# Depthwise inputs stored once per shift, loaded by one transfer for four groups, in a four-layer network on one core

## The chip, the cores and the metric

The kernel runs on one core of one Trainium2 chip. The metric is the device time of one execution in microseconds (us). TensorE (PE) multiplies, VectorE (DVE) does elementwise work and scans, ScalarE (ACT) activations, GpSimd (POOL) issues most DMAs here, and SyncE (SP) issues the rest. Everything is float32.

## The reference

Four layers are applied in a row to x of shape (8, 384, 32, 32).

Layer 0 normalises over channels (RMS norm) and runs a selective state-space block forwards and backwards over the 1024 pixels: an input projection to u and z, a causal depthwise 1-d convolution of u with four taps, then a recurrence with 16 states per channel. Beside it stands a 3x3 depthwise convolution of the normalised image.

```
h = dA * h + dBu;  y = sum over states of h * C        # recurrence, per pixel
local = sigmoid(dwconv3x3(x_norm) + b) * x_norm
x1 = x + res_scale * ((fwd + bwd) * scale_mod + local)
```

Layer 1 is a 1x1 convolution, a 3x3 depthwise convolution, another 1x1 convolution with a residual, linear attention with 8 heads, and an MLP of width 1536. Layers 2 and 3 are sums of depthwise convolutions with up to 13x13 taps, a 1x1 convolution between them, and a GELU at the end.

## The kernel before, in words

**The whole.** A head prepares constants. Then `_layers01` treats layers 0 and 1 image by image (8 images, each in two halves of 512 pixels, 384 channels as three blocks of 128). At the end, layers 2 and 3 run over all images with Toeplitz matrices on PE (L249). The change touches only `_layers01`.

**Depthwise convolutions of layers 0 and 1.** They run on PE. A group is 32 channels; a block of 128 channels has four groups. For a group, an input tile holds the same rows several times, each copy shifted by one element: 32 channels x 3 shifts = 96 partitions for the 3x3 kernel, 32 x 4 = 128 for the 1-d one. A matmul with 32 columns sums the shifted copies with their taps; four groups fill the 128 partitions of one PSUM tile (`col32`, L430). The image goes to a DRAM scratch with a zero border first (`put_image`, L449, into `xn_d` and `h_d`; u into `u_d`, L511). The shifts are made by the load: the source pattern `[1, 3]` reads the same scratch row from three neighbouring starts (`conv3`, L460; for u the pattern `[1, 4]`, L548). So a product of 128 channels needs four loads. Their tiles have the tag `im`, with N_IM = 6 buffers. The scratches have two slots, for even and odd images, and are set to zero once in the head (L372).

**The scan.** `scan(b)` has 48 units per image (2 directions x 2 halves x 3 blocks x 4 groups of states). A unit takes four exponentials on ACT (L682), a product (L695), a scan instruction (L702 or L705) and a second product (L617) on DVE, and four matmuls that sum over the states into `acc` (L619). Its work tiles `du` have four buffers.

**Background work.** `front(b+1)` (norm, projections, depthwise convolutions, step sizes) and `layer1(b-1)` are generators. They are advanced between the units of `scan(b)`, so that PE has work beside DVE. Each `yield n` tells the cost of a step; after unit i the loop has brought the background to `need * (i + 1) / 48`, where `need` is the sum of the numbers given beside each generator: 94 for the front, 290 for layer 1, 30 for folding weights. What is left over when the scan ends is run before the next scan. The yields in the code add up, for the front, to 6 + 36 + 18 + 48 = 108, and for layer 1 to 18 + 18 + 18 + 48 + 4 + 18 + 6 + 6 + 18 + 6 + 6 + 144 = 310.

**Deferred DVE work.** `defer(n, fn)` keeps a piece of DVE work back for n ticks, so that DVE does not wait at once for PE and ACT. `residual` (L790) adds the second 1x1 convolution to the image; `last` (L932) adds the MLP.

**Order and queues.** The program is written with a tile framework. A scheduler in it sets the final order of the instructions on each engine from the order of the code and its own estimates; within an engine that order is kept. All loads and stores of the background go through POOL, in order; each takes one of eight semaphores in turn and waits for the transfer that had it before. The scan's loads go through SP. Weight tiles (`wtile`, L399, tag `w`) have five buffers; activations of half an image (tag `a6`) have seven.

Of the kernel before, what the change touches and what calls it, by code (L numbers as in the profile page):

```python
# [8 lines left out]
FP = mybir.dt.float32  # L9
# [5 lines left out]
P = 128  # L15
C = 384
NC = C // P
H = 32
W = 32
L = H * W  # L20
HALF = 512
# [12 lines left out]
SEG = HALF + 1  # L34
IMG = (H + 2) * (W + 2)

N_A6, N_T2, N_W, N_IM = 7, 10, 5, 6
HIMG = H // 2 * (W + 2)
UL = L + 6


_BN = ["bn1", "bn2", "pw", "dwk", "dw1"] + [f"l2_{j}" for j in range(7)]
# [259 lines left out]
def _layers01(tc, nc, B, xv, x2_d, dram, ident, mean_w, eps5, eps6, one, half, minus1, vec, bns, bnt,  # L302
# [12 lines left out]
    with ExitStack() as ctx:  # L315
# [5 lines left out]
        def scratch(shape, name):  # L321
            return dram.tile(shape, FP, tag=name, name=name)

        x1_d = scratch([B, C, L], "x1_d")
        bc_d = scratch([B, 2, 2 * NST, L], "bc_d")
        xn_d = scratch([2, C, IMG], "xn_d")
        h_d = scratch([2, C, IMG], "h_d")
        u_d = scratch([2, C, UL], "u_d")
        z_d = scratch([B, C, L], "z_d")
        ud_d = scratch([B, C, L], "ud_d")  # L330
        yf_d = scratch([B, C, L], "yf_d")
# [29 lines left out]
            nc.gpsimd.tensor_scalar_mul(dgd[:, c, :], ident, vec("D", c))  # L361


        zero = wp.tile([P, HALF], FP, tag="zero", name="zero")
        nc.gpsimd.memset(zero, 0.0)
        for i in range(2):
            for t, n in ((xn_d, IMG), (u_d, UL), (h_d, IMG)):
                pads = t[i].rearrange("(c p) i -> p c i", p=P)
                for c in range(NC):
                    for a in range(0, n, HALF):  # L370
                        e = min(n, a + HALF)
                        nc.gpsimd.dma_start(pads[:, c, a:e], zero[:, 0 : e - a])  # L372


        das = []
# [31 lines left out]
        late = []  # L407

        def defer(n, fn):
            late.append([n, fn])  # L410

        def tick(everything=False):
            for e in list(late):
# [31 lines left out]

        def put_image(t_d, slot, h, t):

            v = t_d[slot].rearrange("(c p) i -> p c i", p=P)
            nc.gpsimd.dma_start(v[:, :, (W + 2) + HIMG * h : (W + 2) + HIMG * (h + 1)], t)  # L449

        def conv3(t_d, slot, h, c, taps, name):

            ims = []
            for j in range(4):
                im = sp.tile([P, 18 * (W + 2)], FP, tag="im", name=f"{name}_i{j}", bufs=N_IM)
                src = bass.AP(
                    t_d.tensor, t_d[slot, 32 * (4 * c + j), 16 * h * (W + 2)].offset,
                    [[IMG, 32], [1, 3], [1, 18 * (W + 2) - 2]],
                )
                nc.gpsimd.dma_start(im[:96, 0 : 18 * (W + 2) - 2], src)  # L460
                ims.append(im.rearrange("p (h w) -> p h w", w=W + 2))
            ps = psum(name)
            col32(
                ps, lambda j, i: taps[:96, (4 * c + j) * 3 + i, :],
                lambda j, i: ims[j][:96, i : i + 16, 0:W], 3,
            )
            return ps

# [6 lines left out]
        def front(b):  # L475

            xn = []
            for h in range(2):
# [15 lines left out]
                put_image(xn_d, b % 2, h, t)  # L494
                xn.append(mid)
                yield 3
            uo = u_d[b % 2].rearrange("(c p) i -> p c i", p=P)
            for e in range(2):
                w = wtile(inproj_t[:, e * C : (e + 1) * C], f"win_{b}_{e}")
                for h in range(2):  # L500
                    t = a6(f"uz_{b}_{e}_{h}")
                    for m in range(NC):
                        ps = psum(f"in_{b}_{e}_{m}_{h}")
                        dense(ps, w, m, xn[h])
                        if e == 0:
                            nc.scalar.copy(t[:, m, :], ps)  # L506
                        else:
                            nc.scalar.activation(t[:, m, :], ps, AF.Silu)
                        yield 3
                    if e == 0:  # L510
                        nc.gpsimd.dma_start(uo[:, :, 3 + h * HALF : 3 + (h + 1) * HALF], t)  # L511
                    else:
                        nc.gpsimd.dma_start(zv[b][:, :, bass.ts(h, HALF)], t)

# [22 lines left out]
            for h in range(2):  # L537
                cols = bass.ts(h, HALF)
                ucs = [a6(f"uc_{b}_{h}_{d}") for d in range(2)]
                for c in range(NC):  # L540
                    uts = []
                    for j in range(4):
                        ut = sp.tile([P, 18 * (W + 2)], FP, tag="im", name=f"ut_{b}_{h}_{c}_{j}", bufs=N_IM)
                        src = bass.AP(
                            u_d.tensor, u_d[b % 2, 32 * (4 * c + j), h * HALF].offset,
                            [[UL, 32], [1, 4], [1, HALF + 3]],
                        )
                        nc.gpsimd.dma_start(ut[:, 0 : HALF + 3], src)  # L548
                        uts.append(ut)
                    for d in range(2):  # L550
                        ps = psum(f"c1_{b}_{h}_{c}_{d}")
                        col32(
                            ps, lambda j, i: t1[:, d * NG + 4 * c + j, :],
                            lambda j, i: uts[j][:, 3 * d : 3 * d + HALF], 1,
                        )
                        nc.scalar.activation(ucs[d][:, c, :], ps, AF.Silu, bias=vec("conv1d_b", c))
                    yield 2
# [200 lines left out]
        def layer1(b):  # L758
# [22 lines left out]
            w = wtile(c2_d, f"c2_{b}")  # L781
            for h in range(2):
                for m in range(NC):
                    ps = psum(f"c2_{b}_{m}_{h}")
                    dense(ps, w, m, dws[h])
                    t = t2(f"c2_{b}_{m}_{h}")
                    nc.scalar.activation(t, ps, AF.Identity, bias=biasc[:, m, :])

                    def residual(o=xx[h][:, m, :], t=t):
                        nc.vector.tensor_add(o, o, t)  # L790

                    defer(0, residual)
                    yield 3


# [263 lines left out]
```

## Time and profile before

| | |
|---|---|
| median of 3 runs | 6316.81 us (6316.02 to 6326.15) |
| the profiled execution | 6308.41 us, span 6306.2 us |
| mean granted PE clock | 0.888 |
| PE / DVE / ACT / POOL busy | 5329.2 / 3995.1 / 2810.4 / 1001.8 us |
| DMA | 945.57 MB, 150 GB/s over the span |
| head, to the first scan instruction | about 216 us |
| scans of images 0 to 7 | about 216 to 4810 us |
| layer 1 of the last image, alone | about 4810 to 5160 us |
| layers 2 and 3 | about 5160 to 6306 us |

In the profile, a group of instructions is named by its line, engine, and "output<-input" tiles: `dw<-dw_i,t3b` is the depthwise product of layer 1, `lc<-lc_i,t` that of layer 0, `c<-ut,t` the 1-d convolution, `c<-dw,c` the second 1x1 convolution of layer 1, `mf` and `mo` the two matmuls of the MLP, `acc<-du` the scan's sum over states. "PE dw <- DMA dw_i: 17.3, 5, 5.4" reads: PE sat idle before `dw` for 17.3 us in total, 5 times, at most 5.4 us, until that DMA had landed.

### The profile page before, as it was taken

The numbers are of one execution on the slowest core, as the hardware profiler recorded it, in microseconds if no ns is written. First come the engines' busy times: TensorE is split into PE (matmuls) and PEld (weight loads), VectorE is DVE, ScalarE is ACT, GpSimd is POOL, SyncE is SP. The second block draws the span as 40 slices with busy tenths as digits, with TensorE's granted clock in tenths as the row PEclk, the third lists the DMA queues.
The fourth block names the chain that finished last, engine by engine and source line by source line (L and its number), as shares of the span: only waits on it lengthen the run. The fifth ranks groups of instructions, "written<-read, shape, count | busy, mean of one in ns | idle before, by whom it ended". The sixth has DMA issues, their size and how long they took to land. (4 is left out here: it accounts for less than half of the span.)

```text
span 6306.2 us, 52769 instructions
## 1 busy us (share of the span) xinstructions
PE 5329.2 (85%) x18670; PEld 2530.5 (40%) x18670; DVE 3995.1 (63%) x2702; ACT 2810.4 (45%) x3908; POOL 1001.8 (16%) x1608
## 2 busy tenths in 40 slices
PE   4755678987988799879978997898978999999999
PEld 1211213332432243223323332333323449994999
DVE  1699987977796789769877987897895100002000
ACT  1656574556465646655564557454443300002000
POOL 4211130023002201220131012101001010000111
PEclk7776778997998799879988998899888999999999
DMA  7654663456346634653464356445434124445444
GB/s 210 221 184 158 207 222 117 152 191 208 102 154 203 203 100 160 199 182 106 159 228 152 123 165 227 136 145 167 130 109 134 45 72 96 97 92 167 97 95 83
DMA packets 690666, 945.57 MB, mean 150 GB/s; under 512 B 378476, under 2 KB 404260, under 8 KB 690404
## 3 DMA queue, kind: packets, MB, share of 16 engines
q0 software_dynamic: 148784, 542.48, 26.5%
q1 hardware_dynamic: 372912, 377.17, 19.9%
q10 hardware_dynamic: 168708, 22.55, 2.3%
q8 instruction: 149, 2.44, 0.2%
q14 instruction: 113, 0.93, 0.0%
HBM read 715.94 MB, written 226.04 MB: 149 GB/s over the span
## 5 line engine op out<-in xcount | busy, mean ns | idle before, releaser
L682 ACT ACTIVATE da<-dlt,neg_a 128x512 f32<-128x512 f32 x1536 | 1001.9, 713 | 967.3 <-DVE du L705 529.0
L695 DVE TENSOR_TENSOR du<-vr,bct 128x2048 f32<-128x2048 f32 x384 | 874.6, 2284 | 16.3 <-DMA vr<-v_d 10.7
L617 DVE TENSOR_TENSOR du<-du,bct 128x2048 f32<-128x2048 f32 x384 | 877.8, 2287 | 3.8
L702 DVE TENSOR_TENSOR_SCAN du<-da,du 128x2052 f32<-128x2052 f32 x192 | 849.3, 4428 | 37.2 <-ACT da L682 34.3
L705 DVE TENSOR_TENSOR_SCAN du<-da,du 128x2052 f32<-128x2052 f32 x192 | 848.3, 4427 | 6.1
L619 PE MATMUL acc<-du,selt 128*32 128x512 f32 x3072 | 613.4, 696 | 224.0 <-DVE du L617 223.4
L923 PE MATMUL mo<-hm,w 128*128 128x512 f32 x1152 | 547.1, 616 | 53.9 <-ACT hm L921 51.2
L421 PE MATMUL mf<-ln,w 128*128 128x512 f32 x1152 | 547.7, 610 | 0.6 <-DVE ln L909 0.6
L249 PE MATMUL cv_b<-xt_b,toep 128*128 128x240 f32 (+6 forms) x2496 | 488.0, 358 | 10.0 <-DMA xt_b<-xp_d 10.0
L249 PE MATMUL cv_a<-xt_a,toep 128*128 128x240 f32 (+6 forms) x2496 | 487.1, 358 | 0.0
L249 PEld LDWEIGHTS cv_b<-xt_b,toep 128*128 128x128 f32 x2496 | 466.5, 190 | 32.0 <-issue 10.8
L249 PEld LDWEIGHTS cv_a<-xt_a,toep 128*128 128x128 f32 x2496 | 465.8, 190 | 21.1
L430 PE MATMUL c<-ut,t 128*32 128x512 f32 x768 | 245.4, 802 | 146.6 <-ACT dl L581 55.6
L430 PE MATMUL dw<-dw_i,t3b 96*32 96x512 f32 x1152 | 274.9, 852 | 111.7 <-DMA dw_i<-h_d 101.9
L923 PEld LDWEIGHTS mo<-hm,w 128*128 128x128 f32 x1152 | 216.2, 194 | 368.5 <-issue 242.1
L430 PE MATMUL lc<-lc_i,t 96*32 96x512 f32 x1152 | 256.1, 836 | 119.6 <-DMA lc_i<-xn_d 116.3
L421 PEld LDWEIGHTS mf<-ln,w 128*128 128x128 f32 x1152 | 217.7, 194 | 316.5 <-issue 313.1
L619 PEld LDWEIGHTS acc<-du,selt 128*32 128x32 f32 x3072 | 100.4, 116 | 573.7 <-DVE du L617 294.6
L264 DVE COPY yt<-cv_a 128x256 f32<-128x256 f32 x48 | 20.4, 425 | 461.6 <-PE cv_a L249 461.6
L682 ACT ACT_TABLE_LOAD x231 | 296.4, 1283 | 9.2 <-DVE du L702 5.3
L921 ACT ACTIVATE hm<-mf,biasf 128x512 f32<-128x512 f32 x192 | 130.4, 687 | 370.9 <-PE mf L421 370.0
L421 PE MATMUL in<-xn,win 128*128 128x512 f32 x576 | 258.9, 604 | 11.2 <-ACT uz L506 10.0
(207 smaller groups left out, 6044.0 us busy)
## 6 DMA issues: line engine op xcount, KB each, us to landing
dlt<-dl_d SPq DMA_DIRECT2D x384, 256.0 KB, 5.7
vr<-v_d SPq DMA_DIRECT2D x384, 256.0 KB, 4.4
bct<-bc_d SPq DMA_DIRECT2D x256, 256.0 KB, 4.1
ut<-u_d POOLq DMA_DIRECT2D x192, 257.5 KB, 4.8
lc_i<-xn_d POOLq DMA_DIRECT2D x192, 228.8 KB, 5.3
dw_i<-h_d POOLq DMA_DIRECT2D x192, 228.8 KB, 4.5
w<-w_d POOLq DMA_DIRECT2D x64, 576.0 KB, 4.7
w<-in_w POOLq DMA_DIRECT2D x64, 576.0 KB, 4.3
```

Source lines behind the costliest of these rows:

```text
L249: nc.tensor.matmul(pv[:, :, lo:hi], tp[:, kx, :], xg[:, :, lo + s : hi + s], start=(i == 0), stop=(i == KS - 1),)
L264: nc.vector.tensor_copy(hold["t"][:, g % GB, :], ps)
L421: nc.tensor.matmul(ps, w[:, k, m * P : (m + 1) * P], rhs[k] if isinstance(rhs, list) else rhs[:, k, :], start=(k == 0), stop=(k == NC - 1),)
L430: nc.tensor.matmul(ps[32 * j : 32 * j + 32, :], lhs(j, i), rhs(j, i), start=(i == 0), stop=(i == taps - 1), skip_group_check=True,)
L617: nc.vector.tensor_mul(dv, dv, cct[:, 1:2, :].to_broadcast([P, 4, HALF]))
L619: nc.tensor.matmul(acc[32 * j : 32 * j + 32, :], selt, dv[:, j, :], start=False, stop=(r == NR - 1), skip_group_check=True,)
L682: nc.scalar.activation(da[:, SEG * j + 1 : SEG * (j + 1)], dlt[:, j, :], AF.Exp, scale=neg_a[:, 4 * c + j, r : r + 1],)
L695: nc.vector.tensor_mul(flat(1)[:, :, 0:HALF], vt, bct[r][:, 0:1, :].to_broadcast([P, 4, HALF]))
L702: nc.vector.tensor_tensor_scan(du[:, s], da[:, s], du[:, s], 0.0, ALU.mult, ALU.add)
L705: nc.vector.tensor_tensor_scan(du[:, s][:, ::-1], da[:, s][:, ::-1], du[:, s][:, ::-1], 0.0, ALU.mult, ALU.add)
L921: nc.scalar.activation(hm, ps, AF.Gelu, bias=biasf[:, NC * i + f, :])
L923: nc.tensor.matmul(acc[m], wb[:, f, m * P : (m + 1) * P], hm, start=(i == 0 and f == 0), stop=(i == FF // C - 1 and f == NC - 1),)
```

## The change

The scratches get one more dimension, the shift. `put_image` stores an image half three times, each time one element earlier; u is stored four times. A load for 128 channels is then one transfer with four groups in the free dimension, and the tag `im` holds tiles four times as large with two buffers. The zero fill covers the larger scratches with 18 transfers of 12 pieces per partition instead of 54. To make room, weights have four buffers instead of five. The numbers given for the background become 108 and 310. The residual add is deferred by one tick more, and forced before the step that reads it.

```diff
-N_A6, N_T2, N_W, N_IM = 7, 10, 5, 6
+N_A6, N_T2, N_W, N_IM = 7, 10, 4, 2
-UL = L + 6
+UL = L + 8
...
-        xn_d = scratch([2, C, IMG], "xn_d")
-        h_d = scratch([2, C, IMG], "h_d")
-        u_d = scratch([2, C, UL], "u_d")
+        xn_d = scratch([2, C, 3, IMG], "xn_d")
+        h_d = scratch([2, C, 3, IMG], "h_d")
+        u_d = scratch([2, C, 4, UL], "u_d")
...
-        zero = wp.tile([P, HALF], FP, tag="zero", name="zero")
+        zero = wp.tile([P, C + NC + 1], FP, tag="zero", name="zero")
...
-            for t, n in ((xn_d, IMG), (u_d, UL), (h_d, IMG)):
-                pads = t[i].rearrange("(c p) i -> p c i", p=P)
+            for t, n in ((xn_d, 3 * IMG), (u_d, 4 * UL), (h_d, 3 * IMG)):
+                pads = t[i].rearrange("(c p) s i -> p c (s i)", p=P)
                 for c in range(NC):
-                    for a in range(0, n, HALF):
-                        e = min(n, a + HALF)
-                        nc.gpsimd.dma_start(pads[:, c, a:e], zero[:, 0 : e - a])
+                    z = n // 12
+                    nc.gpsimd.dma_start(
+                        pads[:, c, :].rearrange("p (a z) -> p a z", z=z),
+                        zero[:, 0:z].rearrange("p (o z) -> p o z", o=1).to_broadcast([P, 12, z]),
+                    )
...
         def defer(n, fn):
-            late.append([n, fn])
+            e = [n, fn]
+            late.append(e)
+            return e
+
+        def force(e):
+            if e in late:
+                late.remove(e)
+                e[1]()
...
         def put_image(t_d, slot, h, t):
 
-            v = t_d[slot].rearrange("(c p) i -> p c i", p=P)
-            nc.gpsimd.dma_start(v[:, :, (W + 2) + HIMG * h : (W + 2) + HIMG * (h + 1)], t)
+            for e in range(3):
+                v = t_d[slot][:, e].rearrange("(c p) i -> p c i", p=P)
+                at = (W + 2) + HIMG * h - e
+                nc.gpsimd.dma_start(v[:, :, at : at + HIMG], t)
...
-            ims = []
-            for j in range(4):
-                im = sp.tile([P, 18 * (W + 2)], FP, tag="im", name=f"{name}_i{j}", bufs=N_IM)
-                src = bass.AP(
-                    t_d.tensor, t_d[slot, 32 * (4 * c + j), 16 * h * (W + 2)].offset,
-                    [[IMG, 32], [1, 3], [1, 18 * (W + 2) - 2]],
-                )
-                nc.gpsimd.dma_start(im[:96, 0 : 18 * (W + 2) - 2], src)
+            n = 18 * (W + 2)
+            im = sp.tile([P, 4, n], FP, tag="im", name=f"{name}_i", bufs=N_IM)
+            src = bass.AP(
+                t_d.tensor, t_d[slot, P * c, 0, 16 * h * (W + 2)].offset,
+                [[IMG, 96], [96 * IMG, 4], [1, n - 2]],
+            )
+            nc.gpsimd.dma_start(im[:96, :, 0 : n - 2], src)
...
-                        nc.gpsimd.dma_start(uo[:, :, 3 + h * HALF : 3 + (h + 1) * HALF], t)
+                        for q in range(4):
+                            at = 3 + h * HALF - q
+                            uo = u_d[b % 2][:, q].rearrange("(c p) i -> p c i", p=P)
+                            nc.gpsimd.dma_start(uo[:, :, at : at + HALF], t)
...
+                    ut = sp.tile([P, 4, 18 * (W + 2)], FP, tag="im", name=f"ut_{b}_{h}_{c}", bufs=N_IM)
+                    src = bass.AP(
+                        u_d.tensor, u_d[b % 2, P * c, 0, h * HALF].offset,
+                        [[UL, P], [P * UL, 4], [1, HALF + 3]],
+                    )
+                    nc.gpsimd.dma_start(ut[:, :, 0 : HALF + 3], src)
...
-                    defer(0, residual)
+                    res[h].append(defer(1, residual))
...
             for t in range(L // P):
                 h, q = divmod(t, HALF // P)
+                for e in res[h]:
+                    force(e)
...
-                work.append((front(b + 1), 94))
+                work.append((front(b + 1), 108))
...
-                work.append((layer1(b - 1), 290))
+                work.append((layer1(b - 1), 310))
```

More of the change, by code (lines that the diff above doesn't have):

```diff
@@ L446, in put_image @@
         def put_image(t_d, slot, h, t):
-            v = t_d[slot].rearrange("(c p) i -> p c i", p=P)
-            nc.gpsimd.dma_start(v[:, :, (W + 2) + HIMG * h : (W + 2) + HIMG * (h + 1)], t)
+            for e in range(3):
+                v = t_d[slot][:, e].rearrange("(c p) i -> p c i", p=P)
+                at = (W + 2) + HIMG * h - e
+                nc.gpsimd.dma_start(v[:, :, at : at + HIMG], t)
         def conv3(t_d, slot, h, c, taps, name):
-            ims = []
-            for j in range(4):
-                im = sp.tile([P, 18 * (W + 2)], FP, tag="im", name=f"{name}_i{j}", bufs=N_IM)
-                src = bass.AP(
-                    t_d.tensor, t_d[slot, 32 * (4 * c + j), 16 * h * (W + 2)].offset,
-                    [[IMG, 32], [1, 3], [1, 18 * (W + 2) - 2]],
-                )
-                nc.gpsimd.dma_start(im[:96, 0 : 18 * (W + 2) - 2], src)
-                ims.append(im.rearrange("p (h w) -> p h w", w=W + 2))
+            n = 18 * (W + 2)
[5 more added lines that the diff above has]
+            nc.gpsimd.dma_start(im[:96, :, 0 : n - 2], src)
+            iv = im.rearrange("p j (h w) -> p j h w", w=W + 2)
             ps = psum(name)
@@ L464, in conv3 @@
                 ps, lambda j, i: taps[:96, (4 * c + j) * 3 + i, :],
-                lambda j, i: ims[j][:96, i : i + 16, 0:W], 3,
+                lambda j, i: iv[:96, j, i : i + 16, 0:W], 3,
             )
@@ L496, in front @@
                 yield 3
-            uo = u_d[b % 2].rearrange("(c p) i -> p c i", p=P)
             for e in range(2):
@@ L540, in front @@
                 for c in range(NC):
[L541 to L549, printed above, removed]
+                    ut = sp.tile([P, 4, 18 * (W + 2)], FP, tag="im", name=f"ut_{b}_{h}_{c}", bufs=N_IM)
[4 more added lines that the diff above has]
+                    nc.gpsimd.dma_start(ut[:, :, 0 : HALF + 3], src)
                     for d in range(2):
@@ L553, in front @@
                             ps, lambda j, i: t1[:, d * NG + 4 * c + j, :],
-                            lambda j, i: uts[j][:, 3 * d : 3 * d + HALF], 1,
+                            lambda j, i: ut[:, j, 3 * d : 3 * d + HALF], 1,
                         )
@@ L781, in layer1 @@
             w = wtile(c2_d, f"c2_{b}")
+            res = [[], []]
             for h in range(2):
```

## The prediction

> **What bounds the kernel now.** First the page's busy times, then the windows image by image, then one image cut finer, then its waits, and last the head.
>
> ```profile
> PE 5329.2 (85%) x18670; PEld 2530.5 (40%) x18670; DVE 3995.1 (63%) x2702; ACT 2810.4 (45%) x3908; POOL 1001.8 (16%) x1608
> ```
> ```profile
> 0.00:216.00 216.00, 108.62 (x329) 33.77 (x331) 35.25 (x109) 63.96 (x88) 94.31 (x165) 0.78 0.73 227
> 216.00:696.00 480.00, 275.21 (x921) 81.29 (x918) 468.47 (x299) 274.78 (x388) 73.70 (x128) 0.68 0.54 179
> ...
> 2479.00:3092.00 613.00, 522.57 (x1654) 190.55 (x1656) 492.24 (x315) 343.36 (x468) 103.63 (x173) 0.88 0.51 164
> ...
> 4298.00:4810.00 512.00, 435.51 (x1362) 165.71 (x1354) 451.41 (x262) 244.83 (x340) 52.21 (x80) 0.90 0.41 130
> 4810.00:5160.00 350.00, 324.01 (x904) 136.55 (x904) 33.40 (x45) 75.39 (x109) 42.43 (x65) 0.93 0.24 72
> ```
> Columns: window, length, busy PE, PEld, DVE, ACT, POOL, then PE clock, DMA share, GB/s. Scan 0 is DVE alone (468 of 480). Scans 1 to 6 take about 605 each (2479 to 3092 is the fifth, image 4) with PE 522 and DVE 492: neither is full; each waits for the other in turn. (Scan b runs beside the front of image b+1 and layer 1 of image b-1.) A scan unit needs 2.284 + 2.287 + 4.428 = 9.0 us of DVE, 48 units 432; the other 60 are background work, and some 115 to 120 us an image are DVE stalls. Where?
>
> ```profile
> 2508.00:2552.00 44.00, 43.22 (x117) 17.43 (x116) 16.08 (x15) 15.76 (x23) 8.62 (x12) 1.00 0.44 132
> ...
> 2600.00:2640.00 40.00, 26.36 (x115) 6.78 (x117) 31.23 (x23) 19.58 (x22) 9.26 (x17) 0.67 0.77 227
> ...
> 2680.00:2730.00 50.00, 38.64 (x98) 10.70 (x99) 23.08 (x27) 44.30 (x62) 17.70 (x35) 0.73 0.65 229
> ...
> 2780.00:2830.00 50.00, 39.51 (x124) 13.43 (x120) 26.83 (x14) 15.72 (x25) 6.26 (x12) 0.83 0.51 143
> ...
> 2980.00:3030.00 50.00, 44.35 (x112) 17.48 (x110) 48.17 (x26) 27.16 (x35) 5.26 (x7) 0.93 0.35 106
> ```
> ```profile
> PE dw L430 <- DMA dw_i<-h_d: 17.3, 5, 5.4
> PE lc L430 <- DMA lc_i<-xn_d: 16.2, 5, 5.5
> ...
> DVE xx L932 <- PE mo L923: 23.8, 1, 23.8
> ...
> DVE xx L790 <- ACT c L787: 19.9, 6, 10.4
> ```
> Three places. (1) The image's start: PE is full (43.2 of 44) with MLP steps left over from the previous image, and DVE waits 23.8 us in one piece for `mo`. (2) The depthwise stretches, 2600 to 2830: PE has holes of 33 us, waiting for `lc_i` and `dw_i`, at a clock of 0.67 to 0.83. (3) The residual adds. From 2830 on both engines are nearly full. The bare cost of a depthwise product is seen in the last image, where no scan runs:
>
> ```profile
> 4876.66 6.10 PE L430 MATMUL dw<-dw_i,t3b 96*32 96x512 f32 x24 [2.20 <-DMA dw_i<-h_d]
> 4884.15 6.39 PE L430 MATMUL dw<-dw_i,t3b 96*32 96x512 f32 x24 [1.39 <-DMA dw_i<-h_d]
> 4892.32 5.49 PE L430 MATMUL dw<-dw_i,t3b 96*32 96x512 f32 x24 [1.77 <-DMA dw_i<-h_d]
> ```
> A period of 7.7 us: 6.0 of matmul and 1.8 of waiting. The head:
>
> ```profile
> 36.00:78.00 42.00, 4.37 (x6) 1.17 (x4) 2.27 (x4) 5.25 (x8) 34.72 (x65) 0.59 0.88 270
> ```
> ```profile
> 78.56 1.67 ACT L485 ACTIVATE sq<-xi 128x512 f32<-128x512 f32 x3 [28.86 <-DMA xi<-in_x]
> ```
> ```profile
> lc_i<-xn_d POOLq DMA_DIRECT2D x192, 228.8 KB, 5.3
> xn_d<-xn POOLq DMA_DIRECT2D x16, 816.0 KB, 4.1
> xi<-in_x POOLq DMA_DIRECT2D x16, 768.0 KB, 6.2
> xn_d<-zero POOLq DMA_DIRECT2D x12, 256.0 KB, 5.3
> ```
> The zero fill keeps the DMA at 0.88 busy and 270 GB/s; the second half of image 0 (`xi`) is queued behind it on POOL, and ACT idles 28.9 us for it. The head is serial: what lengthens the fill lengthens the run.
>
> **What the Trainium skill says.** DMA: Bandwidth & Descriptors, Anatomy of one DMA: about 2.0 us plus bytes / 436 GB/s. For the new 937 kB load that is an estimate of 4.1; the trace is slower for its neighbours (816 KB store 4.1, 768 KB load 6.2), so I take 5.7. Same page, Issuing engines are not separate DMA queues: POOL's transfers share the 16 engines with SP's, as the head's wait agrees. Same page, Specifications: rows of 512 B and more reach line rate; the new fill has rows of 1156 and 1376 B, which no row here shows. TensorE: Matmul & The Clock Gate, HAM oscillation: DMA waits between matmul groups put the clock back to half; the 0.67 above agrees.
>
> **The change, part by part.**
>
> *Zero fill.* Before: 2 x 384 x (1156 + 1156 + 1030) x 4 B = 10.3 MB in 54 issues. After: 2 x 384 x (3468 + 3468 + 4128) x 4 B = 34.0 MB in 18. The 23.7 MB more at 0.28 MB/us (between the 270 of this window and the 312 GB/s that 180 to 220 us reach) are 85 us. Bounds: 76 at 312, 130 if short rows cost a third. Nothing covers it; in the built program `xi` of half 1 still stands behind all 18.
>
> *Stores.* Two more of each image half (835 kB, xn and h), three more of each u half (786 kB): per image 8 x 0.835 + 6 x 0.786 = 11.4 MB. In the head 8.1 MB of it precede the first product: 29 us of DMA beside 31 us of in-projection on PE; +10 (0 to 29). In the scans, the built order puts three or four units (over 27 us) between stores and loads, so only contention is left: +2 an image, 7 images, +14 (0 to 70). In the last image nothing covers the two more h stores: +6.
>
> *Loads.* 576 become 144. Issue falls from 4 x 0.547 to about 0.77 (the 384-row store). Two buffers hold two whole products; a load starts when the product before the current one ends: 0.8 + 5.7 = 6.5 us against 6.0 us of matmul. The period becomes (6.5 + 6.0)/2 = 6.2 instead of 7.7 or 7.8: 1.6 less, five or six times per run of six. Head -8, last image -8, scan 7 -5. In scans 1 to 6 twelve products give 20 us on PE, but the built order now has all six `lc` products, the six 1-d products of the first half and their projections in one run with no scan matmul (`acc`) between. That run is 6 x 6.2 = 37 for `lc`, 6 x 2.6 = 15 for the 1-d ones (245.4 us over 96 of them in the groups) and about 10 for the projections: 62 us of PE. DVE can go on for four units without an `acc`, since there are four `du` buffers: 36 us, and 8 of small work; then it waits. In the old order `acc` groups stand within this stretch. So I count half: 6 x -10 = -60 (0 to -120). Scan 0 has PE to spare: 0. A load that must wait for its buffer holds up what stands behind it on POOL: stores of the scan and of x1, for which nothing waits soon. Sum -81.
>
> *Counts.* The yields add to 108 for the front and 310 for layer 1, against 94 and 290: 34 of 418 were left over after scans 1 to 6, 20 after scan 7, 14 after scan 0. Removing the pile takes 23.8 us off six image starts: -144. The work is done instead where DVE is full and PE at 0.9: +8 an image (0 to 24), +48. After scan 7, 20 of 310 units of PE work, about 18 us, move under DVE: -15; scan 0, -3. Sum -114.
>
> *Residual adds.* One step later, forced before kv reads them. They stay one run on DVE in the built order, behind the same ACT copies: 0 (-10 to +10 an image).
>
> *Weights.* Four buffers instead of five: the out-projection's weight takes one between MLP pairs, so the next pair's second tile waits for a release; about 2 us an image, +14 (0 to 50). Queued behind it on POOL are stores and the next `xi`, needed later.
>
> Sum: 85 + 10 + 14 + 6 - 81 - 114 + 14 = -66. From the profiled run's 6308.4 (span 6306.2) that is 6242; the median of the runs is 8.4 above it, so 6250.
>
> **Rivals.**
> A (0.40), as summed, 6250; by itself 6170 to 6304.
> B (0.34), slower: the long runs on PE. The `lc` run (units 8 to 12) and the `dw`, `c`, `kv` run (units 19 to 21) leave DVE without `acc` releases. From 11 us of extra stall an image (66/6) the gain is gone; at 22 more, 6250 + 132 = 6382. For it: DVE has only 36 us of buffers. Against: the old order stalls there too (31 of 40, 23 of 50, 27 of 50).
> C (0.20), both gains whole: loads -20 an image and no giving back of the counts: 6250 - 60 - 48 - 40 (adds) = about 6100. For it: DVE's floor is 492.
> D (0.06), the two sides cancel within 0.2% (13 us, about what a measurement of this kernel can tell from no change): 6317.
>
> Faster 0.60 (A and C), same 0.06, slower 0.34. The range 6090 to 6410 reaches from C to past B; A's own is 6170 to 6304.
>
> **What would show it.** Right: image 0's second ACT square moves from 78.6 to about 150 to 165; scan 0 starts about 87 later than 216; no `xx` wait on `mo` at image starts; products in the last image 6.2 apart; scans 1 to 6 near 585. Wrong: head later by over 130; DVE stalls in the `lc` or `dw` run above 40 us; `lc_i` landing above 9 us; PE waiting for `w`.

## The result and the profile after

The changed kernel takes 6488.4 us (6478.6 to 6506.6) against 6316.4 for the kernel before: a ratio of 1.027 (95% interval 1.025 to 1.030), so 2.7% slower. The forecast was 6250 us, with a range of 6090 to 6410. The profiled execution has a span of 6476.8 us, 170.6 more than before.

The busy times say nothing about it: PE is 190 us less busy than before, DVE 14 more, in a span 171 longer.

```profile
PE 5139.5 (79%) x18670; PEld 2481.1 (38%) x18670; DVE 4009.4 (62%) x2702; ACT 2845.6 (44%) x3930; POOL 866.6 (13%) x1252
```

The windows by stage, in the columns used above (window, length, busy PE, PEld, DVE, ACT, POOL, PE clock, DMA share, GB/s), answer to those of before: head, scan 0, the fifth scan (image 4), scan 7, last layer 1.

```profile
0.00:324.00 324.00, 98.47 (x334) 30.84 (x334) 35.33 (x109) 64.00 (x89) 73.09 (x102) 0.90 0.91 248
324.00:799.00 475.00, 272.98 (x952) 82.47 (x952) 465.13 (x301) 265.64 (x382) 66.64 (x106) 0.66 0.61 202
2628.00:3243.00 615.00, 493.11 (x1658) 182.89 (x1658) 494.45 (x314) 348.31 (x470) 88.06 (x133) 0.88 0.57 182
4478.00:4984.00 506.00, 419.51 (x1353) 158.81 (x1351) 454.93 (x265) 254.68 (x348) 46.50 (x66) 0.91 0.44 137
4984.00:5330.00 346.00, 297.75 (x860) 129.20 (x860) 30.41 (x43) 73.11 (x106) 35.99 (x50) 0.91 0.29 81
```

The exact bounds are the starts of the scan instructions in the trace. Between them the 170.6 us divide as follows: head +108 (216 to 324), scan 0 -5, scan 1 +32 (568 to 600), scans 2 to 6 together +45 (a mean of 607 to 616 each), scan 7 -7, and what follows it -3. The loss has two places, the head and scans 1 to 6.

**The head.** Two windows inside the zero fill, and then, from the timeline of ACT, the second group of squares of image 0, which was at 78.6 us before:

```profile
72.00:110.00 38.00, 0.00 (x0) 0.00 (x0) 0.00 (x0) 0.00 (x0) 4.89 (x5) 1.00 1.04 274
110.00:150.00 40.00, 0.00 (x0) 0.00 (x0) 0.00 (x0) 0.00 (x0) 7.08 (x10) 1.00 1.04 263
```
```profile
183.02 1.67 ACT L496 ACTIVATE sq<-xi 128x512 f32<-128x512 f32 x3 [132.04 <-DMA xi<-in_x]
```

All compute engines are idle, the DMA is full, and ACT waits 132.0 us for `xi` where it waited 28.9. The square comes 104.5 us later, which is the fill's share (e2 below takes it away). The rest of the head, from this square to the first scan instruction, takes 141.2 us against 137.5.

**An image in the middle.** First the DVE waits of image 4 (2628 to 3243 us), which answer to the list of before:

```profile
DVE du L702 <- PE acc L629: 38.5, 3, 29.2
DVE du L704 <- PE acc L629: 29.3, 3, 23.0
DVE lg L539 <- ACT lg L536: 14.0, 3, 12.4
DVE dl L602 <- ACT sp L597: 8.5, 3, 4.2
...
DVE xx L801 <- ACT c L798: 7.8, 5, 1.9
```

The 23.8 us for `mo` at the image's start are gone, as forecast. In their place DVE waits 67.8 us for `acc` (38.5 + 29.3), where it waited 29.3 before: the four `du` buffers are all full, and PE doesn't come round to the matmuls that would free them. The timeline of PE shows the longest such stretch, between two groups of `acc` (start, duration, line, tiles, count, and in brackets the idle time before):

```profile
2717.08 1.07 PE L629 MATMUL acc<-du,selt 128*32 128x512 f32 x8 [1.61 <-DVE du L704]
2718.08 0.92 PE L810 MATMUL kvs<-zero 128*128 128x387 f32 x2
2730.89 7.69 PE L440 MATMUL lc<-lc_i,t 96*32 96x512 f32 x48 [11.90 <-issue]
2748.06 7.73 PE L440 MATMUL lc<-lc_i,t 96*32 96x512 f32 x48 [9.48 <-DMA lc_i<-xn_d]
2765.00 7.70 PE L440 MATMUL lc<-lc_i,t 96*32 96x512 f32 x48 [9.22 <-DMA lc_i<-xn_d]
2776.47 5.34 PE L440 MATMUL c<-ut,t 128*32 128x512 f32 x32 [3.77 <-DMA ut<-u_d]
2785.96 2.83 PE L440 MATMUL c<-ut,t 128*32 128x512 f32 x16 [4.15 <-DMA ut<-u_d]
2788.72 6.09 PE L573 MATMUL xd<-uc,wx 128*56 128x512 f32 x12
2794.75 3.69 PE L586 MATMUL dt<-xd,wdt 24*128 24x512 f32 x8
2798.37 1.12 PE L686 MATMUL acc<-y,dgd 128*128 128x512 f32 x2
```

81 us pass from one `acc` to the next. DVE's four free buffers last for four units, about 36 us; in this stretch it stands still for 43 us in all. Two things make the stretch so long. The six `lc` products come in pairs 17 us apart, with 30.6 us of idle PE before them. And behind them, still ahead of the next `acc`, stand the 1-d products, `xd` and `dt`. Call such a stretch on PE a *hole*. In images 2 to 6 of the kernel before, the holes over 40 us are of 45, 57 and 48 us (at units 9, 13 and 21 of the scan). After the change they are of 80, 55 and 58 us.

The issues of the page show why the `lc` products are late. Median time to landing stands in the last column; before, it was 5.3 us for a load of `lc_i` and 4.5 for `dw_i`, each a quarter of the size.

```profile
u_d<-uz POOLq DMA_DIRECT2D x64, 768.0 KB, 10.7
lc_i<-xn_d POOLq DMA_DIRECT2D x48, 915.0 KB, 11.6
dw_i<-h_d POOLq DMA_DIRECT2D x48, 915.0 KB, 7.6
```

Two loads are under way at a time, and the next ones have to wait until PE has read a buffer (POOL's own timeline):

```profile
2719.08 1.37 POOL L471 DMA_DIRECT2D lc_i<-xn_d  x2
2736.32 0.71 POOL L471 DMA_DIRECT2D lc_i<-xn_d  x1 [14.58 <-PE lc L440]
2753.45 0.70 POOL L471 DMA_DIRECT2D lc_i<-xn_d  x1 [13.11 <-PE lc L440]
```

The windows around the hole show how busy the DMA is. (A packet's whole time is counted in the window in which it starts, so a share can exceed 1.)

```profile
2680.00:2700.00 20.00, 20.00 (x56) 7.92 (x56) 15.29 (x12) 9.56 (x15) 8.04 (x11) 1.00 0.98 359
2700.00:2720.00 20.00, 17.38 (x69) 5.93 (x68) 19.58 (x13) 17.12 (x22) 3.93 (x7) 1.00 0.89 326
2720.00:2760.00 40.00, 15.41 (x96) 4.01 (x96) 37.95 (x25) 20.72 (x27) 6.04 (x9) 0.70 1.02 277
```

From 2675 to 2711.8 us the stores of the normalised image and of u are under way. The first `lc` load is issued at 2719.1, behind all of them. In scans 2 to 6 none of the 30 `lc` loads overlaps a store into `xn_d`, `u_d` or `h_d`. What is in flight beside a load is above all the scan's own loads through SP: 6.8 of them (`bct`, `dlt`, `vr`) on average.

### The profile page after: what moved, and what is told of

It reads as the page before. It is cut to its first block, busy times and chain, and to the rows that moved or that the text cites. A ratio compares the mean times of both kernels' runs of the same rounds, so it can differ in the third digit from the quotient of the medians.

```text
span 6476.8 us, 52073 instructions
## 1 busy us (share of the span) xinstructions
PE 5139.5 (79%) x18670; PEld 2481.1 (38%) x18670; DVE 4009.4 (62%) x2702; ACT 2845.6 (44%) x3930; POOL 866.6 (13%) x1252
## 4 chain that ended last, share of the span: by engine, by line
DVE 26%; issue 25%; PE 21%; DMA 8%; ACT 6%; POOL 3%; SPq 1%; DVEq 0%; POOLq 0%; ACTq 0%
DVE du L715 9%; PE cv_a L249 7%; DVE du L705 7%; DVE du L712 5%; DVE du L627 3%; PE c L431 2%; DMA dw_i<-h_d 2%; ACT da L692 2%; DMA lc_i<-xn_d 1%; POOL out L295 1%; PE rzb L890 1%; PE dw L440 1%; DMA ut<-u_d 1%; PE mf L431 1%; PE mo L936 1%
## 5 line engine op out<-in xcount | busy, mean ns | idle before, releaser
L629 PE MATMUL acc<-du,selt 128*32 128x512 f32 x3072 | 524.4, 685 | 268.0 <-DVE du L627 252.7
L936 PE MATMUL mo<-hm,w 128*128 128x512 f32 x1152 | 560.6, 625 | 79.2 <-ACT hm L934 63.4
L440 PE MATMUL lc<-lc_i,t 96*32 96x512 f32 x1152 | 197.9, 834 | 196.4 <-DMA lc_i<-xn_d 125.9
L629 PEld LDWEIGHTS acc<-du,selt 128*32 128x32 f32 x3072 | 80.2, 115 | 613.3 <-DVE du L627 341.2
L440 PE MATMUL dw<-dw_i,t3b 96*32 96x512 f32 x1152 | 195.6, 830 | 124.3 <-DMA dw_i<-h_d 106.6
L440 PE MATMUL c<-ut,t 128*32 128x512 f32 x768 | 140.9, 841 | 178.8 <-DMA ut<-u_d 109.6
L294 ACT ACTIVATE ot<-cv_b,gbias 128x256 f32<-128x256 f32 x96 | 45.4, 473 | 451.8 <-PE cv_b L249 451.8
## 6 DMA issues: line engine op xcount, KB each, us to landing
lc_i<-xn_d POOLq DMA_DIRECT2D x48, 915.0 KB, 11.6
```

Of the source, the lines that this page charges most:

```text
L440: nc.tensor.matmul(ps[32 * j : 32 * j + 32, :], lhs(j, i), rhs(j, i), start=(i == 0), stop=(i == taps - 1), skip_group_check=True,)
L629: nc.tensor.matmul(acc[32 * j : 32 * j + 32, :], selt, dv[:, j, :], start=False, stop=(r == NR - 1), skip_group_check=True,)
L936: nc.tensor.matmul(acc[m], wb[:, f, m * P : (m + 1) * P], hm, start=(i == 0 and f == 0), stop=(i == FF // C - 1 and f == NC - 1),)
```

## The experiments

All times below are medians, with the ratio to the kernel before and its 95% interval. "Image" is the mean length of scans 2 to 6 in the profiled execution (607 us before, 616 after).

**e1: the counts alone.** The kernel before with the two new numbers.

```diff
-                work.append((front(b + 1), 94))
+                work.append((front(b + 1), 108))
-                work.append((layer1(b - 1), 290))
+                work.append((layer1(b - 1), 310))
```

> The kernel before with the two counts alone (108 and 310). Theory P (the pacing costs): in the built order the depthwise products of the norm, six 1-d products and the step-size work of the first half already form one run, as in the changed kernel; a DVE stall of over 40 us stands at units 11 to 12 of scans 2 to 6, it eats the 24 us won at the image start, and the time is 6300 to 6350. Theory S (the storage costs): the pacing alone is a gain, stalls at unit 11 stay under 35 us, scans 2 to 6 fall to about 585 to 590 from 607 and the time to about 6200 to 6230. The head stays at 216 in both.

Measured: 6375.96 us, 1.0089 (1.0066 to 1.0112); the image is 621. The counts alone cost 59 us (77 in the profiled spans), where the prediction had -114. An image's start becomes shorter (units 0 to 6 from 89 to 75 us), but units 6 to 18 grow by 4, 18 to 27 by 8 and 27 to 48 by 17. The DVE waits of image 4, and the hole at unit 8 in the timeline of PE:

```profile
DVE du L692 <- PE acc L619: 43.4, 4, 30.2
DVE du L694 <- PE acc L619: 32.2, 3, 23.0
DVE xx L790 <- ACT c L787: 14.2, 5, 6.7
DVE lg L526 <- ACT lg L523: 9.1, 4, 5.0
...
DVE dl L592 <- ACT sp L587: 5.7, 3, 2.6
```
```profile
2613.73 1.88 PE L619 MATMUL acc<-du,selt 128*32 128x512 f32 x12
...
2658.21 4.47 PE L430 MATMUL lc<-lc_i,t 96*32 96x512 f32 x17 [0.29 <-DMA lc_i<-xn_d]
...
2669.68 5.42 PE L430 MATMUL c<-ut,t 128*32 128x512 f32 x22 [0.44 <-DMA ut<-u_d]
...
2681.16 4.50 PE L563 MATMUL xd<-uc,wx 128*56 128x512 f32 x10
2685.59 3.70 PE L576 MATMUL dt<-xd,wdt 24*128 24x512 f32 x8
2689.21 1.12 PE L676 MATMUL acc<-y,dgd 128*128 128x512 f32 x2
```

The hole at unit 8 is 74 us long on the old storage too. Before, the hole at unit 9 ended after 46 us with 12 of the 48 `c` matmuls of this half in it; now all 48 of them, `xd` and `dt` are ahead of the next `acc`. At unit 21 the hole grows from 50 to 67, by the keys and values (`kv`, `kvs`). So the faster pace groups steps that used to have `acc` between them. That is not the whole loss: the 17 us of units 27 to 48 lie where no hole is (see the second table of the ledger). The median is above both ranges that were expected.

**e2: the zero fill alone taken away.** The changed kernel, with zeros written only where the borders are.

```diff
-            for t, n in ((xn_d, 3 * IMG), (u_d, 4 * UL), (h_d, 3 * IMG)):
...
+            for t in (xn_d, h_d):
+                for s in range(3):
+                    v = t[i][:, s].rearrange("(c p) i -> p c i", p=P)
+                    nc.gpsimd.dma_start(v[:, :, 0 : W + 2 - s], zb[:, :, 0 : W + 2 - s])
...
+            for s in range(4):
+                v = u_d[i][:, s].rearrange("(c p) i -> p c i", p=P)
...
+                nc.gpsimd.dma_start(v[:, :, 3 - s + L : UL], zb[:, :, 0 : UL - L - 3 + s])
```

> The changed kernel with the zero fill cut to what no store covers: the border rows of the images and the few elements before and after u. Theory Z (the 108 us of the head are the zero fill): the first scan instruction comes at about 200 to 235 instead of 324, scans unchanged within 5 us each, and the time falls by 90 to 120 to about 6370 to 6400. Rival: half of it is the other stores of the head, which stay: the first scan instruction at 270, time about 6430.

Measured: 6400.21 us, 1.0123 (1.0099 to 1.0147); 88 us less than with the whole fill. The first scan instruction comes at 224.1 instead of 324.2, the second group of squares at 79.0:

```profile
79.03 1.67 ACT L499 ACTIVATE sq<-xi 128x512 f32<-128x512 f32 x3 [29.00 <-DMA xi<-in_x]
```

The images stay as long as they were (a mean of 620, against 616). The fill explains the head and nothing else; without it the change is still 1.2% slower.

**e3: the storage alone.** The changed kernel with the old counts and the old deferral.

```diff
-                work.append((front(b + 1), 108))
+                work.append((front(b + 1), 94))
-                work.append((layer1(b - 1), 310))
+                work.append((layer1(b - 1), 290))
-                    res[h].append(defer(1, residual))
+                    defer(0, residual)
```

> The changed kernel with the old counts (94 and 290) and the old deferral: the storage, the loads, the fill and the four weight buffers alone. Theory S: loads of the norm's products still land in 11 us or so, scans 2 to 6 get slower than before, 620 to 640, and the time is 6530 to 6600. Theory P: scans 2 to 6 at 590 to 607 and the time 6400 to 6420, that is the head's 108 and little else.

Measured: 6405.91 us, 1.0141 (1.0113 to 1.0168). The head is at 322.3, the image at 602: in the scans the storage gains 5 us an image and about 24 us in all, and the head takes 106. Against this run the full change is 82 us slower, 84 in the profiled spans. So the counts (with the deferral) cost on the new storage about what they cost on the old (59 and 77), and 14 us an image on both.

**e4: the deeper buffers without the stores.** One copy in the scratch and four loads per product as before, but into one tile for the whole product with two buffers; old counts and deferral, four weight buffers.

```diff
-        xn_d = scratch([2, C, 3, IMG], "xn_d")
+        xn_d = scratch([2, C, IMG], "xn_d")
...
-                [[IMG, 96], [96 * IMG, 4], [1, n - 2]],
+                [[IMG, 32], [1, 3], [1, n - 2]],
...
-            nc.gpsimd.dma_start(im[:96, :, 0 : n - 2], src)
+            for j in range(4):
+                nc.gpsimd.dma_start(im[:96, j, 0 : n - 2], src(j))
```

> The kernel before with input tiles for a whole product in two buffers (as in the change, four weight buffers too), but one store per image half, four loads per product, and the old counts. It is the double buffering without the stores. Theory S: loads stay near 5 us, the waits of PE for them fall from about 34 us an image to under 20, scans 2 to 6 at 590 to 600, time 6230 to 6280. If the double buffering itself gains nothing: 6316 within 15. The head stays near 216.

Measured: 6092.54 us, 0.9646 (0.9623 to 0.9669); the image is 572. This is the gain that was hoped for, and 396 us away from the changed kernel. In image 4 (2386 to 2952 us) DVE and PE wait:

```profile
DVE xx L941 <- PE mo L932: 23.8, 1, 23.8
DVE du L700 <- PE acc L625: 22.6, 5, 10.2
DVE du L698 <- PE acc L625: 9.0, 4, 4.0
...
DVE dl L598 <- ACT sp L593: 1.5, 1, 1.5
DVE xx L797 <- ACT c L794: 1.3, 2, 0.9
DVE lg L534 <- ACT lg L531: 0.7, 1, 0.7
```
```profile
PE lc L438 <- DMA lc_i<-xn_d: 5.7, 2, 4.8
PE dw L438 <- DMA dw_i<-h_d: 2.7, 3, 1.5
```

Before, these three last waits of DVE, for what comes out of the depthwise products, were 49.2 us (19.9 + 18.3 + 11.0), and PE waited 33.5 us for `lc_i` and `dw_i`; now it is 3.5 and 8.4. One load's own time to landing has not improved (6.2 us against 5.3). What has changed is how close together the four loads of a product are: from the first issue to the last landing an `lc` product took 14.4 us before and takes 9.2 here (medians of scans 2 to 6). Eight groups fit where six did, and a buffer is now given back for a whole product; the run does not separate the two. The gain is far beyond what was expected (6230 to 6280).

**e5: one store, one load.** e3 with only the unshifted copy stored. The contents of the shifted copies are left out, so the depthwise sums lack two of three (for u, three of four) shifts; the loads read the same bytes.

```diff
-            for e in range(3):
+            for e in range(1):
...
-                        for q in range(4):
+                        for q in range(1):
```

> The storage change with the old counts, but only the unshifted copy of each image half and of u is stored; the loads read the other copies all the same, so what is left out is the content of two of three (three of four) copies, and the output is not the reference's. Theory S (the extra stores make the loads late): lc loads land in about 7 us instead of 12, scans 2 to 6 fall from 602 to about 570, as with deep buffers and single stores, and the time from 6406 to about 6230. Rival G (the one large transfer is late by itself, since it holds four groups and PE needs the first before the last): landing stays above 9 us and the scans above 595.

Measured: 6259.57 us, 0.9908 (0.9890 to 0.9925); the image is 585, `lc_i` lands in 9.4 us. The added stores cost 17 us an image (602 to 585) and 10 us of the head. Neither theory fits: the landing stays above 9 us, as in G, and the image falls below 595.

**e6: three stores, four loads.** e3 with four loads per product.

```diff
-                [[IMG, 96], [96 * IMG, 4], [1, n - 2]],
+                [[IMG, 96], [1, n - 2]],
...
-            nc.gpsimd.dma_start(im[:96, :, 0 : n - 2], src)
+            for j in range(4):
+                nc.gpsimd.dma_start(im[:96, j, 0 : n - 2], src(j))
```

> The storage change with the old counts, all stores, but each product's tile is filled by four loads, one per group. Rival G: a product can begin with the first group, scans 2 to 6 fall to about 575, time 6250 to 6290. Theory S: the stores still fill the DMA, scans 2 to 6 within 10 of 602, time 6380 to 6420.

Measured: 6379.49 us, 1.0094 (1.0077 to 1.0112); the image is 604. With e3 to e5 the four combinations are: one store and four loads 572, one store and one load 585, three stores and four loads 604, three stores and one load 602. The stores cost 17 to 32 us an image. The large load costs 13 with one store and nothing with three. No combination with the large load is better than the four small ones by more than 2 us. What the added stores change in the traces is the order. In e4 and e5, as before, a quarter to a third of an image's `lc` loads are issued before the last store of u has landed, and 24 `acc` matmuls stand between the first and the last `lc` matmul. In e3, e6 and the changed kernel all `lc` loads come behind the stores, and no `acc` stands between the products. The loads there overlap none of these stores, but more of the scan's loads: 6.8 beside a large one in the changed kernel, 2.3 in e5. So the 17 to 32 us come with a changed order; that the stores take bandwidth from the depthwise loads is not seen. Whether they hold back other loads is open.

**e7: e4 with the new counts and the new deferral.**

```diff
-                    defer(0, residual)
+                    res[h].append(defer(1, residual))
-                work.append((front(b + 1), 94))
+                work.append((front(b + 1), 108))
-                work.append((layer1(b - 1), 290))
+                work.append((layer1(b - 1), 310))
```

> Single stores, four loads, whole-product double buffers, with the new counts and the new residual deferral. The counts alone cost 14 us an image and 59 in all on the kernel before. If that cost is PE's own load moved into a stretch where PE is full: here again 8 to 14 us an image in scans 2 to 6, 580 to 588 instead of 573, and 6120 to 6160. If it came from late loads within the front: within 3 us an image, time 6070 to 6095.

Measured: 6168.04 us, 0.9759 (0.9744 to 0.9773); 75 us worse than e4. The image is 587, +15. With early loads the counts lose as much as with late ones. The holes are of 50, 39 and 46 us, where e4's are 39 at most (means over images 2 to 6). The image lies in the range that was expected if PE's own load moves into a stretch where PE is full (580 to 588).

**e8: e4 with the borders alone filled.** The edit of e2, on one copy.

```diff
+            for t in (xn_d, h_d):
+                v = t[i].rearrange("(c p) i -> p c i", p=P)
+                nc.gpsimd.dma_start(v[:, :, 0 : W + 2], zb)
+                nc.gpsimd.dma_start(v[:, :, IMG - (W + 2) : IMG], zb)
```

> Single stores, four loads, whole-product double buffers, old counts, and a zero fill of the borders alone. The head should lose the fill's 37 us (34 to 72 us): the first scan instruction at about 170 instead of 209, scans unchanged, time about 6050 to 6060.

Measured: 6072.59 us, 0.9609 (0.9595 to 0.9624); first scan instruction at 181.6 instead of 208.6. Filling only the borders takes 27 us off the head here too, of the 37 expected; 20 of them are in the median.

**e9: a slower pace.** e8 with a smaller number for layer 1.

```diff
-                work.append((layer1(b - 1), 290))
+                work.append((layer1(b - 1), 256))
```

> Single stores, double buffers, border fill, and the sum of the counts lowered from 384 to 350 (94 and 256), as far below the old sum as the new one is above it; the pile left after a scan doubles to 68 of 418. If what the counts cost lies in the stretch after unit 27, where PE is full (17 us an image for 34 units), a lower sum gives about 17 back there and lengthens the start of the next image by 14 to 17: scans 2 to 6 within 6 us of 574 and the time 6040 to 6110. If only the place of the front's work matters: units 6 to 18 change by over 10 us and the rest does not.

Measured: 6164.94 us, 0.9757 (0.9741 to 0.9774), 92 us worse than e8; the image is 588. Units 27 to 48 take 218 us instead of 223, so the lower sum gives back 5 us there and not the 17 expected. Units 18 to 27 become 14 shorter, but the work left over at the image's start makes one hole of 76 us and 25 us more:

```profile
DVE xx L943 <- PE mo L934: 453.6, 9, 62.3
```

These waits of the whole run were 278.4 us in e8. Of the three sums tried 384 is the best: 350 and 418 both lose 14 us an image, at different ends.

**e10: e7 with the step sizes deferred.** `deltas` (the step `dl`, L598) waited 159.2 us in e7 and 46.2 in e4, so it was a suspect for the counts' loss.

```diff
-                    defer(1, deltas)
+                    defer(3, deltas)
```

> The double-buffered kernel with the new counts, and the step-size work on DVE deferred by three ticks instead of one. In the version with one tick DVE waits 159 us for its ACT input, against 46 with the old counts. If that wait is what units 6 to 12 lose by the counts (15 us an image), they fall from 96 to about 81 to 86 and the time from 6168 to about 6070 to 6110. If the loss is PE's run, which stays: within 20 of 6168.

Measured: 6176.08 us, 0.9774 (0.9755 to 0.9794); no gain over e7. The holes stay at 50, 40 and 47 us. The test is a weak one: these waits fall only from 159.2 to 132.2 us. Units 6 to 12 become 8 us shorter and units 18 to 27 6 us longer, so the loss moved rather than went.

**e11: the same deferral on e8, with the old counts.**

```diff
-                    defer(1, deltas)
+                    defer(3, deltas)
```

> Single stores, double buffers, border fill, old counts, step-size work deferred by three ticks. DVE waits for that work only 46 us with these counts, so little is to be had: 6040 to 6075; more than 30 us of gain would say that the place of the step-size work matters whatever the counts.

Measured: 6026.37 us (6022.41 to 6029.98), 0.9538 (0.9521 to 0.9555): 4.6% faster than before, the best of all runs, with an image of 562 and no hole over 39 us. The deferral gains 10 us an image over e4, and 12 over e8, where it is the only difference: units 18 to 27 fall from 104 to 87 us, units 6 to 18 grow from 158 to 163. The median is 46 us below e8, beyond the 30 that were to say that the place of the step-size work matters whatever the counts; with the new counts (e10) it gained nothing, so it depends on them.

**e12: the kernel before with four weight buffers.**

```diff
-N_A6, N_T2, N_W, N_IM = 7, 10, 5, 6
+N_A6, N_T2, N_W, N_IM = 7, 10, 4, 6
```

> The kernel before with four weight buffers instead of five, nothing else. The prediction put 14 us on it (0 to 50): 6330. If the fifth buffer was not needed: 6316 within 10.

Measured: 6316.67 us, 1.0000 (0.9988 to 1.0012). The buffer taken from the weights costs nothing.

## The ledger of image 4

The DVE waits of image 4 by what they wait for, from the lists of waits; all in us. "Depthwise" sums the waits of `dl`, `lg` and the residual add; the last column is the length of the scan less all the waits.

| run | `mo` at the start | `acc` | depthwise | others | scan | rest |
|---|---|---|---|---|---|---|
| before | 23.8 | 29.3 | 49.2 | 15.1 | 613.0 | 496 |
| e3, storage | 23.8 | 30.3 | 38.9 | 15.8 | 604.9 | 496 |
| e6, four loads | 23.8 | 30.6 | 38.6 | 16.3 | 605.2 | 496 |
| e5, one store | 23.8 | 32.5 | 16.1 | 18.1 | 586.2 | 496 |
| e4, deeper buffers alone | 23.8 | 31.6 | 3.5 | 11.6 | 566.2 | 496 |
| e1, counts | 0 | 75.6 | 29.0 | 19.4 | 623.7 | 500 |
| after | 0 | 67.8 | 30.3 | 17.8 | 615.4 | 500 |
| e7, e4 with counts | 0 | 44.5 | 23.4 | 21.2 | 586.9 | 498 |
| e9, slower pace | 48.8 | 24.2 | 12.2 | 10.2 | 589.8 | 494 |
| e11 | 23.8 | 23.8 | 2.5 | 18.1 | 563.9 | 496 |

An image is 494 to 500 us of DVE work plus what DVE waits. The storage acts on the depthwise column: 49 to 39 with the added stores, to 3.5 with the deeper buffers alone. The counts take away the 24 for `mo`. In e1 they add 46 of `acc` and take 20 off the depthwise column; in e7 they add 13 of `acc` and 20 of depthwise waits. The other waits and the rest grow too, by 5 to 12 together.

The second table shows where in an image the time lies: mean lengths of four stretches of units in scans 2 to 6, from the starts of the scan instructions, in us.

| run | units 0 to 6 | 6 to 18 | 18 to 27 | 27 to 48 | image |
|---|---|---|---|---|---|
| before | 88.9 | 181.0 | 114.0 | 223.1 | 607 |
| e1, counts | 74.9 | 184.5 | 121.6 | 239.8 | 621 |
| e3, storage | 88.9 | 184.2 | 106.6 | 222.0 | 602 |
| after | 72.8 | 186.9 | 118.4 | 237.8 | 616 |
| e4, deeper buffers alone | 88.8 | 157.7 | 103.9 | 222.0 | 572 |
| e7, e4 with counts | 72.6 | 169.8 | 106.0 | 238.6 | 587 |
| e8, e4 with borders | 88.9 | 157.8 | 104.0 | 223.4 | 574 |
| e9, slower pace | 113.7 | 165.4 | 90.4 | 218.2 | 588 |
| e11 | 88.9 | 162.9 | 87.3 | 223.0 | 562 |

In all three pairs (e1 and before, after and e3, e7 and e4) the counts make the start 14 to 16 us shorter, units 6 to 27 11 to 15 longer, and units 27 to 48 16 to 17 longer. In these runs the holes over 40 us lie in units 6 to 27. In units 27 to 48 no stretch without `acc` passes 19 us with the new counts, less than the 23 of before. What is added there is the work that used to be left over: 27 `mf` and 27 `mo` matmuls an image, while some of the key and value matmuls move ahead of unit 27. In e1 PE is busy 11 us longer there (202 to 213), and DVE waits 15 us longer (11 to 26), for `acc`, for `rzb` in the attention and for a load of z.

## Why the prediction was wrong

**The step that failed is the counts.** They were put at -114 and cost +59 alone (e1), +82 on the new storage together with the deferral (after against e3). The removal itself was right: the wait on `mo` at the starts is gone, though the start becomes only 14 to 16 us shorter and not 24. Wrong was the price of the work given back, "+8 an image", taken from how full PE and DVE are on average (0.9). It is +28 to +31, so that an image is 14 to 15 us longer instead of 16 shorter.

Somewhat less than half of this price lies in units 6 to 27. There the trace shows steps of the background between two `acc` groups for longer than the 36 us that four `du` buffers last; the faster pace put the 1-d products, `xd` and `dt` behind the `lc` run. The larger part, 16 to 17 us, lies in units 27 to 48, where the work left over now runs. It is not a matter of long holes, and no run separates its causes: e9, with less work there, got 5 us back.

The prediction's own paragraph on the loads had found the `lc` run in the built order (62 us of PE against 36 + 8), and then set it against the loads alone and counted "half". The trace shows 81 us. Two of the forecast's signs of being wrong came true here: DVE stalls in the `lc` run above 40 us (43 in all), and `lc_i` landing above 9 us (11.6).

**Loads and stores: nearly right in sum, by the luck of errors that cancel.** For the scans the terms were -65 for loads, +14 for stores, +14 for weights, so -37; e3 has about -24. But the gain from the deeper buffers is -35 an image (e4), not -10, and the stores' price was +17 to +32, not +2. That the stores are over when the loads start was right. What was mis-sized is the load. It was put at 5.7 us, from neighbours in the trace, above the estimate of 4.1 us worked out from the Trainium skill's DMA: Bandwidth & Descriptors, Anatomy of one DMA. It took 11.6 us in the changed kernel and 9.4 with one store (e5), so here the measurement decides. That POOL's and SP's transfers share the DMA engines agrees with these loads, which take longer beside 6.8 of the scan's loads than beside 2.3; the head's wait for `xi` doesn't show it, since `xi` and the fill are both POOL's. The product period in the `lc` run was then not 6.2 us but 17 for two.

**Zero fill: mechanism right, size off.** 85 forecast, 104.5 measured at image 0's second group of squares; 23.7 MB in 104.5 us are 0.227 MB/us instead of 0.28. The rows of 1156 and 1376 B themselves moved at 263 to 274 GB/s in the two windows shown, about the 270 of before. The bounds 76 to 130 held. The rest of the head was put at +2 and is +4.

**Weights** were +14 and are 0 (e12). **Scan 0** was -3 and is -5; the last image, with layers 2 and 3, was -2 and is -3; **scan 7** was -20 beside its start, for loads and the moved pile, and is -7 in all.

From -66 to +171 in the profiled spans are 237 us. The counts are 198 of them (-114 to +84, e3's span to that of the changed kernel), the fill 19, the storage in the scans 13, the rest 7. (The prediction's "about 605 each" fits scans 2 to 6, whose mean was 607; scan 1 took 568.)

**Rival B**, with 0.34, named one of the two right places: long runs on PE without `acc`, at the `lc` run and at the `dw`, `c`, `kv` run. It did not name units 27 to 48. Its 6382 took the forecast's head and 22 us of extra stall an image from the order of the loads. The runs put the head 21 us higher, and show that the counts lengthen these runs even with the old loads (e1). Rival C, both gains whole at 6100, is about what e4 reaches (6093), but without the counts and without the stores.

**What stays open.** The deferral of the residual add was run only together with the counts. An image loses 14 us by the counts without it (e1) and 14 to 15 with it, so it can be little in the scans. Why the scheduler joins just these steps at the faster pace was not followed further, and no run changes the order alone, so its share of the price is read from the traces. What makes units 27 to 48 longer, and how the added stores lead to the later loads, were not separated.

## What to carry to other kernels

When background work is fed between the units of a pipeline, look in the trace for the longest stretch in which the feeding engine doesn't serve the pipeline, and hold it against the time that the pipeline's buffers last; moving work earlier gains nothing if it lengthens that stretch. Then price the moved work where it lands, stretch by stretch, and not by how full the engines are on average. Split a change before judging it: here the deeper buffer was worth 3.5%, and the stores, the fill and the counts that came with it cost 6%. When copies are made in DRAM so that loads become fewer, look in the built order at where the added stores put the loads, and at what else is in flight then.

## What was unexpected in the hardware

One load of 915 KB was no faster than four of 229 KB issued in a row. From the first issue to the last landing, an `lc` product took 8.8 us with the one load (e5; 9.4 over the whole run) and 9.2 with four (e4), both medians of scans 2 to 6. With four, PE began a product 1.2 us before its last load had landed, with one 1.5 us after; with the same single store the image was 13 us longer with the one load. That the earlier start is the cause agrees with this, but is not shown by itself.

With the DMA share at 0.98 to 1.04, what it moved differs: 359 GB/s at 2680 to 2700 us, among the stores, 277 at 2720 to 2760, with the loads, and 263 to 274 in the zero fill. In these windows a full DMA is not one rate, so an estimate from bytes and one rate can be off by a quarter. Which transfers lower the rate was not tested.
